# Another order of work in a hand-ordered attention pipeline

## The chip, the core and the metric

The kernel runs on one core of a Trainium2 chip. The metric is the device time of one execution in microseconds (us). Four engines compute: TensorE (PE; its weight loads are PEld), VectorE (DVE), ScalarE (ACT) and GpSimd (POOL). SyncE (SP) issues transfers. Matrix products land in PSUM, which has eight banks here; DVE and ACT read it, and everything else lives in SBUF. Each engine runs its own instructions in the order written and waits for the others by semaphores.

## What is computed

A model of four blocks over an input of 4 sequences of 512 tokens with 128 features, in fp32. The first three (a gated scan, a mixture of eight experts, a causal attention) are not touched. The last is six layers, each a local attention with 16 heads of 64 features, in windows of 32 tokens with the window before, and a feed-forward block. Cut to what matters:

```python
def attn_layer(x, Wqkv, qs, ksc, Wo):          # x: 4 x 512 x 128
    q, k, v = jnp.split(x @ Wqkv, 3, -1)       # to 16 heads of 64
    q = l2norm(q) * qs
    k = l2norm(k) * ksc
    q = q * cos * scale + rotate_half(q) * sin * scale
    k = k * cos * inv + rotate_half(k) * sin * inv
    sim = einsum(q, k) * 8                      # own window and the one before
    attn = softmax(where(mask, -max, sim))
    return einsum(attn, v) @ Wo

def ffn_layer(x, g, bln, W1, b1, W2, b2):
    xn = (x - mean) / sqrt(var + 1e-5) * g + bln
    a, gate = jnp.split(xn @ W1 + b1, 2, -1)    # 341 features each
    return a * gelu(gate) @ W2 + b2

for i in range(6):
    x = attn_layer(x, ...) + x
    x = ffn_layer(x, ...) + x
```

## The kernel before

The six layers are one stage. Its unit of work is a `Chunk`: 128 tokens of one sequence in one layer, 6 x 4 x 4 = 96 of them in the order layer, sequence, chunk. A chunk passes through five iterations of the loop at the end of `fused`: as `xe` it gets its queries, keys and values, as `xd` its scores and exponentials, as `xc` its weighted values, as `xb` the transposes of these, as `xa` the output product. So each iteration works on five chunks at once. The order of the calls in the loop is the order on every engine: after the loop each instruction is tied to the one before it on its engine.

What the calls do, with the names of the tiles as the profile shows them:

- `rotate(j)`, four times a chunk (j = 0, 1: queries, 2, 3: keys): one product `q` (128 x 512), on DVE two multiplications by the rotation's tables (`lt`, L547 and L551), on POOL their sum `ro`, on ACT the square `sq` (L558), on DVE its sums over each head `ss` (L559). `scale_keys` and `scale_queries` turn the sums into the factors `rk` and `rn` by a power on POOL (L569); the keys are multiplied by theirs there (L576).
- `window` and `turn(j, engine)`: the transposes `tp_r` of a rotated piece into `qT` or `kT`, with a copy out of PSUM.
- `scores(g)`, for two groups of eight heads: the mask as a product with the identity (L621) and the scores `ls` onto it (L630), the largest of each row `lm` (L637) and its scaled form `lnb` (L641).
- `exponentials(g, of)`: eight activations `lp` (L650).
- `flip(g, k, engine)`: four transposes `lpt` of the exponentials and a copy `lpT`.
- `weigh(g)`: the weighted values `lo` (L674), a reciprocal `lr`, and the division `on` (L680, L682).
- `lift(j)`: transposes `tp_on` and the copy `oT`.
- `values(j)`: the product `lv` and its copy `vr` on ACT. `spread` sends `vr` to `vk` by three transfers on SP.
- `project`: the output product `ly` (L698), added to the sequence `sA` on DVE (L704).

After the fourth chunk of a sequence its `feedforward` is put on a list; `advance()` in the loop runs it piece by piece over the next four iterations: transposes `tp_f`, a copy `fn` and the norm's statistics `st_f`, `mv_f`, `rs_f` (L115 to L118), then the normalisation (L123), then transposes `tp_fb` and `xn`, the gates `fg`, the other half `fa` in three steps, the output `fy`. The number k of the iteration says which of these fall into it.

PSUM is shared out by tags, with two tiles each: `mm` (one bank each: `q`, `lv`, `ly`, `fa`, `fy` and one gate), `tr` (one bank each: all transposes) and `S` (two banks each: `ls`, `lo` and two gates). A new tile takes a bank when the tile before it in that bank has been read. [...]

Of the kernel before, what the change touches and what calls it, by code (L numbers as in the profile page):

```python
# [66 lines left out]
def fused(ctx: ExitStack, tc: tile.TileContext, a: dict, out: bass.AP):  # L67
# [7 lines left out]
    def psum(tag, name):  # L75
        return pp.tile([P, 2, 512] if tag == "S" else [P, 512], F32, tag=tag, name=name)
# [10 lines left out]
    def chunks(x):  # L87
        return x.rearrange("p (c d) -> p c d", c=NC)
# [360 lines left out]
    with ExitStack() as stage:  # L449
# [68 lines left out]
        class Chunk:  # L518


            def __init__(self, n, l, b, c, w, last):
                self.l, self.b, self.c, self.w, self.last = l, b, c, w, last
                self.tag = f"{l}_{b}_{c}"
                self.xs = sA[b][:, c * P : (c + 1) * P]
                self.V = vr[n % 2]
                self.VK = vk[n % 2]
                self.ss = sm.tile([P, 2 * HEADS], F32, tag="ss", name=f"ss{self.tag}")
                self.rot = {}
                self.S = {}
                self.nb = {}  # L530
                self.P = {}
                self.pT = {}
                self.on = {}

            def rotate(self, j):

                tag = f"{self.tag}_{j}"
                q = psum("mm", f"q{tag}")
                nc.tensor.matmul(  # L539
                    q, lhsT=self.xs, rhs=self.w["qkv"][:, j * 512 : (j + 1) * 512],  # L540
                    start=True, stop=True,
                )
                cs = self.w["rot"][:, 2 * (j // 2), self.c, :]
                sn = self.w["rot"][:, 2 * (j // 2) + 1, self.c, :]
                t1 = wk.tile([P, 512], F32, tag="t1", name=f"lt1{tag}")
                t2 = wk.tile([P, 512], F32, tag="t2", name=f"lt2{tag}")
                nc.vector.tensor_tensor(  # L547
                    heads(t1), heads(q), cs[:, None, :].to_broadcast([P, 8, DH]), ALU.mult
                )
                sn = sn.rearrange("p (two d) -> p two d", two=2)  # L550
                nc.vector.tensor_tensor(  # L551
                    swapped(t2), swapped(q)[:, :, ::-1, :],
                    sn[:, None].to_broadcast([P, 8, 2, 32]), ALU.mult,
                )
                self.rot[j] = wk.tile([P, 512], F32, tag="rotd", name=f"ro{tag}", bufs=6)
                nc.gpsimd.tensor_tensor(self.rot[j], t1, t2, ALU.add)  # L556
                sq = wk.tile([P, 512], F32, tag="sq", name=f"sq{tag}")
                nc.scalar.activation(sq, q, AF.Square)  # L558
                nc.vector.tensor_reduce(  # L559
                    self.ss[:, j * 8 : j * 8 + 8], heads(sq), AX.X, ALU.add  # L560
                )

            def norms(self, j, name, square):
# [49 lines left out]
                    to = self.kT[:, 4 * j - 8 : 4 * j - 4, WIN:]  # L613
                move(engine, to, chunks(tp))

            def scores(self, g):

                gt = f"{self.tag}_{g}"
                S = psum("S", f"ls{gt}")[:, :, 0 : 4 * KB]
                for par in range(2):  # L620
                    nc.tensor.matmul(  # L621
                        S[:, par], lhsT=ident_h, rhs=bands[min(self.c, 1)], start=True, stop=False
                    )
                S = S.rearrange("p a (s k) -> p a s k", s=4)
                for s in range(4):
                    for blk in range(2):

                        for par in range(2):
                            lo, to = par * 64, blk * QB
                            nc.tensor.matmul(  # L630
                                S[to : to + QB, par, s, :],
                                lhsT=self.qT[lo : lo + 64, 4 * g + s, to : to + QB],
                                rhs=self.kT[lo : lo + 64, 4 * g + s, to : to + KB],
                                start=False, stop=s == 3,
                            )
                m = sm.tile([P, 4, 2], F32, tag="lm", name=f"lm{gt}")
                nc.vector.tensor_reduce(  # L637
                    m.rearrange("p s a -> p a s"), S, AX.X, ALU.max, negate=True
                )
                nb = sm.tile([P, 8], F32, tag="lnb", name=f"lnb{gt}")  # L640
                nc.vector.tensor_tensor(  # L641
                    nb, m.rearrange("p s a -> p (s a)"), self.rq[:, 8 * g : 8 * g + 8], ALU.mult
                )
                self.S[g], self.nb[g] = S, nb
# [22 lines left out]
            def weigh(self, g):  # L667
                gt = f"{self.tag}_{g}"
                o = psum("S", f"lo{gt}")[:, :, 0 : 4 * (DH + 1)]
                o = o.rearrange("p a (h d) -> p a h d", h=4)  # L670
                for i in range(8):
                    for blk in range(2):
                        to = blk * QB
                        nc.tensor.matmul(  # L674
                            o[to : to + QB, i // 4, i % 4, :],
                            lhsT=self.pT[g][:, i, to : to + QB],
                            rhs=self.VK[blk][:, 8 * g + i, :], start=True, stop=True,
                        )
                r = sm.tile([P, 2, 4], F32, tag="lr", name=f"lr{gt}")
                nc.vector.reciprocal(r, o[:, :, :, DH])  # L680
                self.on[g] = wk.tile([P, 512], F32, tag="on", name=f"on{gt}", bufs=4)
                nc.vector.tensor_tensor(  # L682
                    self.on[g].rearrange("p (a h d) -> p a h d", a=2, h=4), o[:, :, :, 0:DH],
                    r[:, :, :, None].to_broadcast([P, 2, 4, DH]), ALU.mult,
                )
# [8 lines left out]
            def project(self):  # L694
# [7 lines left out]
                for h in range(2):  # L702
                    to = half(self.b, h)[:, self.c * P : (self.c + 1) * P]
                    nc.vector.tensor_tensor(to, y[h * 64 : h * 64 + 64, :], to, ALU.add)  # L704

        def feedforward(l, b, w):

# [68 lines left out]
        def advance():  # L776
            if steps:
                try:
                    next(steps[0])
                except StopIteration:  # L780
                    steps.pop(0)

        def at(i):
            return made[i] if 0 <= i < len(made) else None

        for i in range(len(todo) + 4):
            if i < len(todo):
# [6 lines left out]
            if xd:  # L794
                xd.window()
            if xc:
                xc.flip(0, 0, nc.vector)
            if xe:
                xe.rotate(2)
            if xc:  # L800
                xc.flip(0, 1, nc.scalar)
            if xa:
                xa.project()
                if xa.c == NC - 1:
                    steps.append(feedforward(xa.l, xa.b, xa.w))
                k = (xa.c + 1) % NC
            if xd:
                xd.turn(2, nc.scalar)
            if xe:
                xe.rotate(3)  # L810
                xe.scale_keys()
            if xd:
                xd.turn(0, nc.scalar)
            if xc:
                xc.weigh(0)
            if xb:
                xb.lift(0)
            if xd:
                xd.scores(0)
            if xe:  # L820
                xe.rotate(0)
            if xd:
                xd.exponentials(0, range(8))
            if xc:
                xc.flip(1, 0, nc.vector)
            if k in (0, 2):
                advance()
            if xc:
                xc.flip(1, 1, nc.vector)
            advance()  # L830
            if xd:
                xd.turn(3, nc.scalar)
            if xe:
                xe.rotate(1)
                xe.scale_queries()
            if xd:
                xd.turn(1, nc.scalar)
            if xc:
                xc.weigh(1)
            if xb:  # L840
                xb.lift(1)
            if xd:
                xd.scores(1)
            if xe:
                xe.values(0)
            if xd:
                xd.exponentials(1, range(4))
            if k in (0, 2):
                advance()
            if xe:  # L850
                xe.values(1)
                xe.spread()
            if xd:
                xd.exponentials(1, range(4, 8))
        while steps:
            advance()

# [111 lines left out]
```

## Time and profile before

| | |
|---|---|
| median of 3 runs | 3016.34 us (3015.14 to 3021.13) |
| the profiled execution | 3016.47 us |
| its span, first to last instruction | 3014.7 us |
| mean granted TensorE clock | 0.933 of full speed |
| busy PE, DVE, ACT, POOL | 2558.3, 1950.1, 1476.6, 1401.7 us |
| first `ly` addition of the six layers | at 825.6 us |
| last `ly` addition | at 2974.7 us |

The table is read so: the layers take over two thirds of the span, and the 95 intervals between their first and last output products are 22.6 us each on average. Busy time counts an engine's instructions from start to end; for PE, whose products overlap, it is no measure of how much more it could do.

### The profile page before, as it was taken

To read this page: it belongs to the slowest core of one execution; us is meant where nothing else is said; L and a number is where in the kernel's file an instruction comes from. 1 tells how busy PE (TensorE), PEld (TensorE's weight loads), DVE (VectorE), ACT (ScalarE), POOL (GpSimd) and SP (SyncE) were. 2 spreads that over 40 slices of the span, in tenths; PEclk is the share of its full clock that TensorE was granted. 3 is DMA by queue.
4 is the path that set the end of the run, shared out by engine and by line. 5 is a ranking of instruction groups with operands and counts; after the bars stand their busy time and mean duration, and the time that the engine had idled before them with its cause. 6 is when DMAs were issued, how large, how long until landed. Compare 5 with 4: busy or idle time off the path is not lost.

```text
span 3014.7 us, 56751 instructions
## 1 busy us (share of the span) xinstructions
PE 2558.3 (85%) x22640; PEld 1679.1 (56%) x22640; DVE 1950.1 (65%) x4218; ACT 1476.6 (49%) x3417; POOL 1401.7 (46%) x1002
## 2 busy tenths in 40 slices
PE   3899888887779888888888898888888888988886
PEld 1567545554456555555555565555555555655553
DVE  6344466666676666766667666666666676666764
ACT  1111133333556555555555565555555555655553
POOL 2000011111766555665556555565655565555550
PEclk7799989999899999999999999999999999999998
DMA  5000000000112111121112111121111211111110
GB/s 168 1 1 1 1 1 1 1 1 1 42 32 77 32 31 33 42 67 33 31 40 67 33 42 31 31 68 41 32 32 32 75 34 31 41 32 31 37 37 17
DMA packets 44963, 103.92 MB, mean 34 GB/s; under 512 B 5526, under 2 KB 23196, under 8 KB 43804
## 3 DMA queue, kind: packets, MB, share of 16 engines
q1 hardware_dynamic: 41852, 97.27, 12.3%
q8 instruction: 178, 2.92, 0.4%
q10 hardware_dynamic: 2848, 3.03, 0.3%
q14 instruction: 85, 0.70, 0.1%
HBM read 25.75 MB, written 1.05 MB: 9 GB/s over the span
## 4 chain that ended last, share of the span: by engine, by line
PE 33%; DVE 22%; ACT 17%; issue 2%; ACTq 0%; DMA 0%; DVEq 0%; POOL 0%; POOLq 0%
PE q L539 7%; PE ly L698 6%; ACT lp L650 6%; PE lv L586 5%; DVE lt L547 5%; ACT sq L558 5%; PE tp_r L134 4%; DVE lt L551 4%; DVE ss L559 3%; PE ls L630 3%; DVE lm L637 3%; DVE on L682 2%; PE lo L674 2%; PE lpt L662 2%; PE tp_on L134 1%
## 5 line engine op out<-in xcount | busy, mean ns | idle before, releaser
L556 POOL TENSOR_TENSOR ro<-lt,lt 128x512 f32<-128x512 f32 x384 | 487.5, 1270 | 721.8 <-DVE lt L551 369.3
L558 ACT ACTIVATE sq<-q 128x512 f32<-128x512 f32 x384 | 232.1, 604 | 644.8 <-DVE lt L551 603.1
L650 ACT ACTIVATE lp<-ls,lnb,rn 128x96 f32<-128x96 f32 x1536 | 529.0, 450 | 4.1 <-DVE lnb L641 3.8
L559 DVE TENSOR_REDUCE ss<-sq 128x8 f32<-128x512 f32 x384 | 263.3, 686 | 352.4 <-ACT sq L558 352.4
L539 PE MATMUL q<-wqkv,sA 128*128 128x512 f32 x768 | 430.5, 644 | 4.7 <-DVE fh L738 2.9
L134 PEld LDWEIGHTS tp_r<-ident,ro 128*128 128x128 f32 x1536 | 197.6, 151 | 265.4 <-issue 156.0
L547 DVE TENSOR_TENSOR lt<-q,rot 128x512 f32<-128x512 f32 x384 | 265.4, 691 | 106.4 <-PE q L539 105.0
L134 PE MATMUL tp_r<-ident,ro 128*128 128x128 f32 x1536 | 254.8, 293 | 81.9 <-DVE st_f L115 48.1
L662 PEld LDWEIGHTS lpt<-ident,lp 128*96 128x96 f32 x1536 | 180.6, 130 | 242.3 <-issue 139.6
L569 POOL TENSOR_TENSOR rn<-rn,neg_half 128x16 f32<-128x16 f32 x96 | 278.9, 2905 | 64.9 <-DVE rn L566 64.8
L569 POOL TENSOR_TENSOR rk<-rk,neg_half 128x16 f32<-128x16 f32 x96 | 278.8, 2905 | 27.6 <-DVE rk L566 27.6
L662 PE MATMUL lpt<-ident,lp 128*96 128x128 f32 x1536 | 233.4, 282 | 64.0 <-DVE lpT L516 60.8
L551 DVE TENSOR_TENSOR lt<-q,rot 128x512 f32<-128x512 f32 x384 | 261.0, 680 | 0.0
L516 DVE COPY lpT<-lpt 96x512 f32<-96x512 f32 x288 | 192.0, 681 | 105.6 <-PE lpt L662 105.5
L630 PE MATMUL ls<-kT,qT 64*64 64x96 f32 x6144 | 185.7, 262 | 53.7 <-ACT qT L516 53.7
L674 PE MATMUL lo<-vk,lpT 96*64 96x65 f32 x6144 | 223.8, 225 | 1.1 <-ACT lpT L516 1.1
L630 PEld LDWEIGHTS ls<-kT,qT 64*64 64x64 f32 x6144 | 149.8, 142 | 128.3 <-issue 65.5
L698 PE MATMUL ly<-oT,lwo 128*128 128x128 f32 x1536 | 194.4, 280 | 26.9 <-ACT vr L590 26.9
L674 PEld LDWEIGHTS lo<-vk,lpT 96*64 96x64 f32 x6144 | 197.0, 138 | 35.7 <-issue 34.3
L586 PE MATMUL lv<-wqkv,sA 128*128 128x512 f32 x384 | 207.4, 644 | 3.2 <-ACT sq L558 3.2
L590 ACT COPY vr<-lv 128x512 f32<-128x512 f32 x192 | 113.8, 593 | 179.4 <-PE lv L586 179.4
L698 PEld LDWEIGHTS ly<-oT,lwo 128*128 128x128 f32 x1536 | 178.9, 192 | 37.8 <-ACT vr L590 32.5
(178 smaller groups left out, 4195.8 us busy)
## 6 DMA issues: line engine op xcount, KB each, us to landing
vk<-vr SPq DMA_DIRECT2D x96, 390.0 KB, 4.0
vk<-vr SPq DMA_DIRECT2D x96, 260.0 KB, 3.4
vk<-vr SPq DMA_DIRECT2D x72, 130.0 KB, 2.3
wqkv<-in_lwqkv_dram SPq DMA_DIRECT2D x6, 1536.0 KB, 10.0
ew<-in_ew_dram SPq DMA_DIRECT2D x16, 256.0 KB, 6.3
lwo<-in_lwo_dram SPq DMA_DIRECT2D x6, 512.0 KB, 10.9
lw<-in_lw_dram SPq DMA_DIRECT2D x6, 341.0 KB, 10.2
cst<-in_cst_dram ACTq DMA_DIRECT2D x1, 1028.0 KB, 5.3
```

Of the source, the lines that this page charges most:

```text
L134: nc.tensor.transpose(tp[:, c * P : (c + 1) * P], i[:, c, :], ident)
L539: nc.tensor.matmul(q, lhsT=self.xs, rhs=self.w["qkv"][:, j * 512 : (j + 1) * 512], start=True, stop=True,)
L547: nc.vector.tensor_tensor(heads(t1), heads(q), cs[:, None, :].to_broadcast([P, 8, DH]), ALU.mult)
L551: nc.vector.tensor_tensor(swapped(t2), swapped(q)[:, :, ::-1, :], sn[:, None].to_broadcast([P, 8, 2, 32]), ALU.mult,)
L556: nc.gpsimd.tensor_tensor(self.rot[j], t1, t2, ALU.add)
L558: nc.scalar.activation(sq, q, AF.Square)
L569: nc.gpsimd.tensor_tensor(r, r, neg_half.to_broadcast([P, HEADS]), ALU.pow)
L630: nc.tensor.matmul(S[to : to + QB, par, s, :], lhsT=self.qT[lo : lo + 64, 4 * g + s, to : to + QB], rhs=self.kT[lo : lo + 64, 4 * g + s, t ...
L650: nc.scalar.activation(self.P[g][:, i, :], self.S[g][:, i % 2, i // 2, :], AF.Exp, bias=self.nb[g][:, i : i + 1], scale=self.rq[:, 8 * g + ...
L662: nc.tensor.transpose(pt[0:KB, i * P : (i + 1) * P], self.P[g][:, 4 * k + i, :], ident)
L674: nc.tensor.matmul(o[to : to + QB, i // 4, i % 4, :], lhsT=self.pT[g][:, i, to : to + QB], rhs=self.VK[blk][:, 8 * g + i, :], start=True, ...
L698: nc.tensor.matmul(y, lhsT=self.w["o"][:, j, :], rhs=self.oT[:, j, :], start=j == 0, stop=j == INNER // P - 1,)
```

## The change

The loop calls the same work in another order, and several functions are cut in two so that their halves can be called apart.

- `rotate` is cut: `query(j)` does the product and its square, `rotate(j)` the rest. The square is now ahead of the two multiplications, and `query(3)` is called between `rotate(2)` and `rotate(3)`, ahead of `project`.
- `scores` is cut into `mask`, `scores` and `largest`; `weigh` into `weigh` and `divide`. The mask's product, the weighted values and the scores are called one after the other, and `lift` follows them. The mask's tile is now taken before that of the weighted values.
- `project` follows `turn(0)`. It puts the feed-forward on the list itself.
- The norm's statistics read the copy `fn` in SBUF, no longer `tp_f` in PSUM.
- The engine of the copies of `flip` and `turn(3)` depends on k. Over four iterations DVE had twelve copies of `flip` and ACT four; now DVE has nine and ACT seven. One of the four copies of `turn(3)` is on DVE.
- The second product of the values and all exponentials of the second group are at the end of the iteration.

```diff
-            def rotate(self, j):
+            def query(self, j):
                 tag = f"{self.tag}_{j}"
-                q = psum("mm", f"q{tag}")
+                self.q[j] = q = psum("mm", f"q{tag}")
                 nc.tensor.matmul(
                     q, lhsT=self.xs, rhs=self.w["qkv"][:, j * 512 : (j + 1) * 512],
                     start=True, stop=True,
                 )
+                self.sq[j] = wk.tile([P, 512], F32, tag="sq", name=f"sq{tag}")
+                nc.scalar.activation(self.sq[j], q, AF.Square)
+
+            def rotate(self, j):
+                tag, q = f"{self.tag}_{j}", self.q[j]
...
                 nc.gpsimd.tensor_tensor(self.rot[j], t1, t2, ALU.add)
-                sq = wk.tile([P, 512], F32, tag="sq", name=f"sq{tag}")
-                nc.scalar.activation(sq, q, AF.Square)
                 nc.vector.tensor_reduce(
-                    self.ss[:, j * 8 : j * 8 + 8], heads(sq), AX.X, ALU.add
+                    self.ss[:, j * 8 : j * 8 + 8], heads(self.sq[j]), AX.X, ALU.add
                 )
...
-            def scores(self, g):
-                gt = f"{self.tag}_{g}"
-                S = psum("S", f"ls{gt}")[:, :, 0 : 4 * KB]
+            def mask(self, g):
+                self.S[g] = S = psum("S", f"ls{self.tag}_{g}")[:, :, 0 : 4 * KB]
                 for par in range(2):
                     nc.tensor.matmul(
                         S[:, par], lhsT=ident_h, rhs=bands[min(self.c, 1)], start=True, stop=False
                     )
-                S = S.rearrange("p a (s k) -> p a s k", s=4)
+
+            def scores(self, g):
+                self.S[g] = S = self.S[g].rearrange("p a (s k) -> p a s k", s=4)
...
+            def largest(self, g):
+                gt, S = f"{self.tag}_{g}", self.S[g]
                 m = sm.tile([P, 4, 2], F32, tag="lm", name=f"lm{gt}")
...
+            def divide(self, g):
+                gt, o = f"{self.tag}_{g}", self.o
                 r = sm.tile([P, 2, 4], F32, tag="lr", name=f"lr{gt}")
...
-            stats = statistics(chunks(tp), f"f{tag}")
+            stats = statistics(n, f"f{tag}")
...
-            xa, xb, xc, xd, xe = (at(i - k) for k in (4, 3, 2, 1, 0))
-            k = (i - 4) % NC
...
+            xa, xb, xc, xd, xe = (at(i - k) or idle for k in (4, 3, 2, 1, 0))
+            k = (i - 3) % NC
+            xd.window()
+            xc.flip(0, 0, nc.vector)
+            xe.query(2)
+            xc.flip(0, 1, nc.vector if k in (1, 3) else nc.scalar)
+            xd.turn(2, nc.scalar)
+            xe.rotate(2)
+            xe.query(3)
+            xd.turn(0, nc.scalar)
+            xa.project()
+            xe.rotate(3)
+            xe.scale_keys()
+            xd.mask(0)
+            xc.weigh(0)
+            xc.divide(0)
+            xd.scores(0)
+            xd.largest(0)
+            xb.lift(0)
+            xe.query(0)
+            xd.exponentials(0, range(8))
+            xe.rotate(0)
             if k in (0, 2):
                 advance()
+            xc.flip(1, 0, nc.scalar if k in (0, 2) else nc.vector)
             advance()
+            xc.flip(1, 1, nc.vector if k == 1 else nc.scalar)
+            xd.turn(3, nc.vector if k == 1 else nc.scalar)
+            xe.query(1)
+            xd.turn(1, nc.scalar)
+            xe.rotate(1)
+            xe.scale_queries()
             if k in (0, 2):
                 advance()
+            xe.values(0)
+            xd.mask(1)
+            xc.weigh(1)
+            xc.divide(1)
+            xd.scores(1)
+            xd.largest(1)
+            xb.lift(1)
+            xe.values(1)
+            xe.spread()
+            xd.exponentials(1, range(8))
```

The removed loop had, for an iteration with all five chunks and without the tests for missing ones: `xd.window`, `xc.flip(0, 0, DVE)`, `xe.rotate(2)`, `xc.flip(0, 1, ACT)`, `xa.project`, `xd.turn(2)`, `xe.rotate(3)`, `xe.scale_keys`, `xd.turn(0)`, `xc.weigh(0)`, `xb.lift(0)`, `xd.scores(0)`, `xe.rotate(0)`, `xd.exponentials(0, 0..7)`, `xc.flip(1, 0, DVE)`, `advance` for k = 0 and 2, `xc.flip(1, 1, DVE)`, `advance`, `xd.turn(3)`, `xe.rotate(1)`, `xe.scale_queries`, `xd.turn(1)`, `xc.weigh(1)`, `xb.lift(1)`, `xd.scores(1)`, `xe.values(0)`, `xd.exponentials(1, 0..3)`, `advance` for k = 0 and 2, `xe.values(1)`, `xe.spread`, `xd.exponentials(1, 4..7)`; all `turn`s with ACT's copies. An iteration without some chunk skipped its calls by tests; in the changed loop an empty `Idle` object takes them.

More of the change, by code (lines that the diff above doesn't have):

```diff
@@ L527, in __init__ @@
                 self.ss = sm.tile([P, 2 * HEADS], F32, tag="ss", name=f"ss{self.tag}")
+                self.q = {}
+                self.sq = {}
                 self.rot = {}
@@ L643, in scores @@
                 )
-                self.S[g], self.nb[g] = S, nb
+                self.nb[g] = nb
                 self.P[g] = wk.tile([P, 8, KB], F32, tag="lp", name=f"lp{gt}")
@@ L669, in weigh @@
                 o = psum("S", f"lo{gt}")[:, :, 0 : 4 * (DH + 1)]
-                o = o.rearrange("p a (h d) -> p a h d", h=4)
+                self.o = o = o.rearrange("p a (h d) -> p a h d", h=4)
                 for i in range(8):
@@ L704, in project @@
                     nc.vector.tensor_tensor(to, y[h * 64 : h * 64 + 64, :], to, ALU.add)
+                if self.c == NC - 1:
+                    steps.append(feedforward(self.l, self.b, self.w))
         def feedforward(l, b, w):
@@ L781, in advance, with __getattr__ @@
                     steps.pop(0)
+        class Idle:
+            def __getattr__(self, name):
+                return lambda *of: None
+        idle = Idle()
         def at(i):
@@ L791, in fused @@
                 made.append(Chunk(i, l, b, c, ws[l], at(i - 1)))
-            xa, xb, xc, xd, xe = (at(i - k) for k in (4, 3, 2, 1, 0))
-            k = (i - 4) % NC
[L794 to L825, printed above, removed]
+            xa, xb, xc, xd, xe = (at(i - k) or idle for k in (4, 3, 2, 1, 0))
@@ L826, in fused @@
+            xb.lift(0)
+            xe.query(0)
+            xd.exponentials(0, range(8))
+            xe.rotate(0)
             if k in (0, 2):
                 advance()
-            if xc:
-                xc.flip(1, 1, nc.vector)
+            xc.flip(1, 0, nc.scalar if k in (0, 2) else nc.vector)
             advance()
[L831 to L847, printed above, removed]
+            xc.flip(1, 1, nc.vector if k == 1 else nc.scalar)
[4 more added lines that the diff above has]
+            xe.scale_queries()
@@ L848, in fused @@
             if k in (0, 2):
                 advance()
[L850 to L854, printed above, removed]
+            xe.values(0)
[8 more added lines that the diff above has]
+            xd.exponentials(1, range(8))
         while steps:
```

## The prediction

> **What bounds the kernel now.** I read the page's busy shares and slices first, then the busy times by stretch, then the waits, then the timeline. The stage that the change touches runs from about 780 us to the end, 96 chunks of tokens, and is even: slices 11 to 39 look alike.
>
> ```profile
> PE 2558.3 (85%) x22640; PEld 1679.1 (56%) x22640; DVE 1950.1 (65%) x4218; ACT 1476.6 (49%) x3417; POOL 1401.7 (46%) x1002
> ...
> PEclk7799989999899999999999999999999999999998
> ```
>
> TensorE is the fullest engine, yet not at its limit. The stretches show four chunks in a row, cut at the starts of `ls` of group 1 (columns: length, then busy PE, PEld, DVE, ACT, POOL, then the granted clock):
>
> ```profile
> 1523.83:1548.70 24.87, 19.56 (x205) 13.54 (x205) 17.17 (x41) 12.73 (x31) 14.39 (x11) 0.86 0.12 30
> 1548.70:1571.86 23.16, 20.81 (x212) 13.54 (x211) 14.64 (x31) 16.04 (x35) 13.43 (x11) 0.97 0.15 36
> 1571.86:1594.63 22.77, 20.24 (x206) 13.37 (x205) 15.09 (x27) 12.94 (x31) 12.86 (x9) 0.96 0.12 30
> ```
>
> With the chunk before them (1502.46 to 1523.83, 21.37 us) four chunks, a "round", take 92.17 us, and every round repeats it: the same transposes start at 1447.71, 1539.87 and 1632.02. I name the chunks by the k of the loop: k=0 (the feed-forward's norm) 24.87, k=1 (its gates) 23.16, k=2 (its other half) 22.77, k=3 (its output) 21.37. Who stops TensorE, from the waits of 1000 to 2900 us (total, times, longest):
>
> ```profile
> PE lpt L662 <- DVE lpT L516: 55.2, 20, 2.8
> PE tp_r L134 <- DVE st_f L115: 43.1, 19, 2.3
> PE ls L630 <- ACT qT L516: 39.3, 126, 0.6
> PE tp_on L134 <- ACT kT L516: 36.8, 20, 1.8
> PE ly L698 <- ACT vr L590: 25.7, 21, 1.3
> ```
>
> So once a round TensorE waits 2.8, 2.3, 1.8 and 1.3 us, and at most chunks' scores 0.3. Each long wait has a tail. The timeline of PE (start, length, tile, then the wait before it):
>
> ```profile
> 1536.07 0.60 PE L662 MATMUL lpt<-ident,lp 128*96 128x128 f32 x4
> 1536.51 0.60 PE L134 MATMUL tp_f<-ident,sA 128*128 128x128 f32 x4
> 1539.87 1.09 PE L662 MATMUL lpt<-ident,lp 128*96 128x128 f32 x4 [2.76 <-DVE lpT L516]
> 1543.23 1.09 PE L134 MATMUL tp_r<-ident,ro 128*128 128x128 f32 x4 [2.27 <-DVE st_f L115]
> 1544.11 1.92 PE L539 MATMUL q<-wqkv,sA 128*128 128x512 f32 x2
> 1545.82 0.96 PE L134 MATMUL tp_r<-ident,ro 128*128 128x128 f32 x4
> 1546.71 1.15 PE L674 MATMUL lo<-vk,lpT 96*64 96x65 f32 x32
> ...
> 1552.22 1.02 PE L539 MATMUL q<-wqkv,sA 128*128 128x512 f32 x2
> ```
>
> Four transposes take 0.60 us when PE has run on (`lpt` at 1536.07) and 1.09 after the wait, a `q` pair 1.02 and 1.92: half speed, until about 1546.4, shortly before `lo`. After the round's 1.84 us (up to 1570.28) it comes again, until about 1573.8; after its 1.27 us (up to 1578.57) it does not.
>
> [...] `sq` (L558) reads the `q` that L551 reads, and waited for it 603.1 us in all. [...] The trace has 0.53 us from the start of `tp_r` to that of `lo` (another mode) against 0.43 from `tp_r` to `q` (the same): about 0.1 a change.
>
> **The change part by part.** Durations below are start to start, from the timeline of 1500 to 1595 us: DVE's 512-wide operations 0.61 (0.69 to their end), `lm` 1.05, `lr` 0.23, eight exponentials 2.52, `sq` 0.63 until DVE goes on, `lv` to its copy 1.16, `q` to its square 1.13; PE: `tp_on` 0.50, `tp_r` 0.45 (0.53 ahead of `lo`), `q` 0.86, `lv` 0.88, `ly` 1.88, mask 0.44, `lo` 1.09, `ls` 0.82.
>
> *Squares first.* DVE's wait `ss <- sq` goes (15.0 us in the waits of one round). But now L547 can only start when `sq` is done, and `sq` of piece 2 stands in ACT's order behind the eight exponentials of group 1. The banks of the changed program, as built, say who waits for that: `ly`, moved behind `rotate(2)`, lies in the bank of that `q`; before, it lay in the bank of `lv`. From the end T of a chunk's last `ls`: `lv` starts at 0.50, its copy at 1.66, the exponentials at 2.14 (`lnb` is there at 1.6), `sq` at 4.66, L547 at 5.29, L551 from 5.90 to 6.58, **`ly` at 6.65**. TensorE has had only 4.93 us of work by then (0.50, 0.88, `lpt` 0.44, `q` 0.86, `lpt` 0.44, `tp_r` 0.45, `q` 0.86, `tp_r` 0.50): a **new wait of 1.2 to 1.7 us in every chunk** (where ACT copies the second half of `lpT`, k even, most of it falls on the `tp_r` ahead of `ly`, whose bank that copy, queued behind the square, must free). Queued behind `ly`: all of PE, and on DVE its two additions, then everything.
>
> *From `ly` on* DVE sets the pace. `ly` ends its issue at 8.53, DVE adds at 8.75 (0.55), rotates piece 3 (3 x 0.61), `rk` 0.17, `lr` and `on` 0.84, `lm` at 12.12, `lnb` 13.17, rotates piece 0 from 13.28 (1.83), copies `lpT` at 15.11, done 15.80. `tp_r` of piece 3 needs that bank: 15.87. Then `tp_r` 0.45, `q` 0.86, `tp_r` 0.53, `lv` 0.88, mask 0.44, `lo` 1.09, `ls` 0.82: 5.07, so k=3 ends at **20.94**. Its feed-forward product (2.6) hides: PE is free at 15.73.
>
> *Copies dealt by turn.* k=1 has three of them on DVE, so ACT goes from exponentials (13.51 to 16.19) to the table load 1.28 and three gates at 0.6: 19.3; `lv` takes their bank then, +3.23: **22.6**. k=2: `lpT` on ACT behind the exponentials, 16.03 to 16.60; `tp_r` 16.67, `q` 17.12, its square 18.25, L547 and L551 until 20.17; `lv`, in that `q`'s bank, at 20.24: **23.5**.
>
> *Norm from SBUF.* k=0: `fn` is copied behind the exponentials at 16.03; the bank is free at 16.66 and no longer after 1.92 us more of statistics. Reading SBUF costs the same (`st_z` 268 ns, `st_f` 274). But PE waits from 13.1 to 16.7 for `fn`, and statistics until 18.6, POOL's power 1.02, L123 1.12, end 20.97, then `tp_fb` and 3.23: **24.4**.
>
> *Mask, weighted values, scores side by side.* The wait for `qT` (1.9 us in that round) goes: `qT` is there at 7.5, `ls` starts at 10.1. One mode change in four goes, 0.1 each, and of it only the second group's lies on the chain: under 0.4 a round, within my rounding. POOL has 13.3 us a chunk of 22 and is early everywhere (`ro` of piece 0 ends at 18.0, wanted in the next chunk); SP issues the same three transfers behind the same `vr`, at 2.3, and `lo` wants them two chunks on: nothing, unless they came a whole chunk late.
>
> Sum: 24.4 + 22.6 + 23.5 + 20.9 = **91.4 against 92.17**, but at full clock, where the 92.17 holds two half-clock stretches. It is a floor for these durations: each term is a chain in the engines' written order. What the half clock adds I can only bound. Below, 0: the waits at `ly` are 1.2 to 1.7, between the 1.27 that was not throttled and the 1.84 that was. Above, 7.5: all four `ly` at half speed, 1.88 each. k=0's wait of 3.6 is throttled for sure, but the norm covers it. I take 1.7 a round, as one `ly` in four at half speed costs 1.9 and some of it falls after `ly` where DVE is later anyway: 93.1, +0.9 x 23 rounds = +21, and +3 for the four chunks before any feed-forward, which take 20.19 now and 20.9 to 21.5 then. On the profiled execution's 3016.47 us (its span 3014.7; the median of the runs is 3016.34): **3040 us**.
>
> **Rivals.** (1) Not slower: the clock holds at `ly`. Then 91.4: 3016.5 - 0.8 x 23 + 3 = 3001 us. For it: 1.27 us never throttled; the side is decided where the half clock costs 0.7 us a round, a third of one `ly`. Against: 1.7 is nearer 1.84. (2) No change: [...] In the trace of before the first wait of the rounds comes at 987.26, 1079.25, 1171.32, 1263.44 and so on: 91.99, 92.07, 92.12 apart, then 92.15 and no more, [...] 3017 to 3020. (3) Every `ly` at half speed: 98.9, about 3175. (4) PE runs dense: the round less its 11.3 us of listed waits, 23 x 11.3 = 260, gives 2757. For it: 15 us of DVE's waits go. Against: the chain through `sq` and `ly` is longer than such a round.
>
> **Numbers.** Forecast slower, 3022 to 3090: 0.4; (3) and what lies between: 0.1; (2) 0.17; (1), my sums being up to 1.5% too long: 0.31; (4) 0.02. 0.2% is about what a measurement of this kernel tells from no change. Range 2985 to 3110: it leaves out a tenth above and less below.
>
> **What would show it.** Right: a wait `ly <- DVE lt` of over 1 us in nearly every chunk, `ss <- sq` and `st_f` gone, `tp_r <- lpT` or DVE in its place, rounds of 91 to 95 us. Wrong: `ly` without a wait, or rounds under 90.

## The result, and the profile after

| | before | after |
|---|---|---|
| median | 3016.57 us | **3118.26 us** (3115.35 to 3122.05, 4 runs) |
| ratio | | 1.0335, 95% interval 1.0317 to 1.0353 |
| the profiled execution, its span | 3016.47, 3014.7 us | 3122.05, 3119.9 us |
| mean granted clock | 0.933 | 0.945 |
| first to last addition of `ly` | 2149.1 us | 2252.1 us |

The change makes the kernel 3.4% slower, and nearly all of it lies in the layers: their interval is 103.0 us longer, the whole span 105.2. (The median of before holds one run more than the table ahead.) The forecast was 3040 us, with a range up to 3110. The page after, busy shares and granted clock:

```profile
PE 2519.2 (81%) x22640; PEld 1667.1 (53%) x22640; DVE 2025.8 (65%) x4170; ACT 1521.5 (49%) x3465; POOL 1402.8 (45%) x1002
...
PEclk7799898999999999999999999999999999999898
```

TensorE is less full than before (2519.2 us busy against 2558.3) and its clock is higher (0.945 against 0.933), so the loss is waiting, not slower products. From one start of `tp_f` to the next a round took 91.83 to 92.18 us before, 92.13 on average over the first twenty. After, it takes 95.47 to 95.49 in most rounds (95.48 below) and 97.2 or 97.6 in some, 96.13 on average: +4.0, and these twenty rounds are 80 of the 105 us. Busy times by stretch of one typical round after, cut as in the prediction, for k=0, 1, 2, 3 (length, busy PE, PEld, DVE, ACT, POOL, granted clock, DMA share, GB/s):

```profile
1559.99:1584.88 24.89, 19.32 (x213) 13.66 (x209) 17.55 (x39) 14.56 (x33) 14.98 (x11) 0.93 0.13 33
1584.88:1608.15 23.27, 19.60 (x209) 12.84 (x206) 16.02 (x30) 14.24 (x31) 12.56 (x10) 1.00 0.14 36
1608.15:1633.89 25.74, 19.81 (x211) 12.70 (x207) 16.91 (x29) 14.58 (x32) 15.00 (x11) 1.00 0.11 27
1633.89:1655.48 21.59, 19.11 (x210) 12.88 (x206) 16.09 (x28) 12.27 (x29) 11.37 (x9) 1.00 0.15 38
```

No chunk got its forecast (24.4, 22.6, 23.5, 20.94); k=2 is off by most. The granted clock is 1.00 in three of the four and 0.93 in k=0. The rounds of 97.2 and 97.6 differ from this one in k=2 (27.47 and 27.12) and in the k=0 between them (25.63); k=1 and k=3 are the same in every round. TensorE's waits of 1000 to 2900 us after (total, times, longest):

```profile
PE tp_r L134 <- ACT lpT L516: 83.7, 59, 2.7
PE lpt L672 <- ACT fn L726: 81.5, 20, 4.1
PE ly L711 <- ACT qT L516: 69.6, 40, 1.8
PE fa L750 <- DVE lt L558: 32.4, 20, 1.8
PE lv L591 <- ACT fh L744: 29.8, 20, 1.5
```

The long waits of before (`lpt` for `lpT`, `tp_r` for `st_f`, `tp_on` for `kT`) are no longer among them, and new ones stand behind ACT: `tp_r` three times a round, `ly` twice, `lpt` once for `fn`. Now the middle of k=3 after, one round earlier, from the timeline of all engines (start, length, engine, line; then the wait before it):

```profile
1545.15 0.68 DVE L558 TENSOR_TENSOR lt<-q,rot 128x512 f32<-128x512 f32 x1
...
1545.97 2.02 PE L711 MATMUL ly<-oT,lwo 128*128 128x128 f32 x16 [1.77 <-ACT qT L516]
...
1548.04 0.59 DVE L717 TENSOR_TENSOR sA<-ly,sA 64x128 f32<-64x128 f32 x2 [1.61 <-PE ly L711]
...
1549.87 0.68 DVE L564 TENSOR_REDUCE ss<-sq 128x8 f32<-128x512 f32 x1
1550.10 1.27 POOL L563 TENSOR_TENSOR ro<-lt,lt 128x512 f32<-128x512 f32 x1 [2.85 <-DVE lt L558]
...
1550.58 0.82 DVE L571 TENSOR_SCALAR rk<-ss 128x16 f32<-128x16 f32 x1
...
1551.31 0.20 DVE L693 RECIPROCAL lr<-lo 128x8 f32<-128x8 f32 x1
```

`ly` starts 6.75 us after the chunk's start (T = 1539.22), where 6.65 was forecast, after a wait of 1.77. The view names `qT`, which `ly` does not read; L558, the last reader of the bank that `ly` takes, ends at 1545.83, 0.06 before that copy. (That `ly` waits for the bank follows from the order in which the tiles are taken; the view alone does not show it.) DVE then waits 1.61 for `ly`. And `rk`, 174 to 177 ns in every instance before, takes 0.82: it ends at 1551.40, when POOL's `ro` ends (1551.37). So it is in 95 of the 96 chunks: `rk` ends 0.03 us after the `ro` beside it. The same place before:

```profile
1512.52 0.60 ACT L558 ACTIVATE sq<-q 128x512 f32<-128x512 f32 x1 [1.73 <-DVE lt L551]
...
1513.15 0.69 DVE L559 TENSOR_REDUCE ss<-sq 128x8 f32<-128x512 f32 x1 [0.72 <-ACT sq L558]
...
1513.87 0.17 DVE L566 TENSOR_SCALAR rk<-ss 128x16 f32<-128x16 f32 x1
```

There DVE stood 0.72 us before `ss`. POOL's `ro` ran from 1512.57 to 1513.84, in that wait and beside `ss`, and `rk` found it over. The wait that the change was credited with removing had covered `ro`. With the square done early `ss` follows L558 at once, and `rk` comes while `ro` still runs.

In k=2, ACT's timeline shows what else is late:

```profile
1513.65 0.59 ACT L595 COPY vr<-lv 128x512 f32<-128x512 f32 x1 [0.28 <-PE lv L591]
1514.25 1.28 ACT L660 ACT_TABLE_LOAD   x1
1515.55 2.69 ACT L660 ACTIVATE lp<-ls,lnb,rn 128x96 f32<-128x96 f32 x8
1518.09 0.64 ACT L546 ACTIVATE sq<-q 128x512 f32<-128x512 f32 x1
1518.57 0.60 ACT L516 COPY lpT<-lpt 96x512 f32<-96x512 f32 x1
```

The chunk before used Gelu, and a table load of 1.28 us stands ahead of the eight exponentials (in e2, without Gelu, it is gone); the square and the copy `lpT` behind them come that much later, and `tp_r` waits 2.67 for that copy.

### The profile page after: what moved, and what is told of

It is laid out like the page before. It is cut to its first block, busy times and chain, and to the rows that moved or that the text cites. A ratio compares the mean times of both kernels' runs of the same rounds, so it can differ in the third digit from the quotient of the medians.

```text
span 3119.9 us, 56778 instructions
## 1 busy us (share of the span) xinstructions
PE 2519.2 (81%) x22640; PEld 1667.1 (53%) x22640; DVE 2025.8 (65%) x4170; ACT 1521.5 (49%) x3465; POOL 1402.8 (45%) x1002
## 4 chain that ended last, share of the span: by engine, by line
PE 30%; ACT 22%; DVE 21%; issue 3%; POOL 0%; DMA 0%; DVEq 0%; ACTq 0%; POOLq 0%
ACT lp L660 13%; PE ly L711 7%; PE lv L591 6%; DVE lt L554 4%; DVE lt L558 4%; PE lo L684 3%; PE q L541 3%; PE tp_r L134 3%; DVE lm L647 3%; ACT sq L546 3%; PE ls L636 3%; DVE rk L571 2%; DVE ss L564 2%; DVE on L695 2%; PE tp_on L134 2%
## 5 line engine op out<-in xcount | busy, mean ns | idle before, releaser
L660 ACT ACTIVATE lp<-ls,lnb,rn 128x96 f32<-128x96 f32 x1536 | 517.3, 445 | 98.5 <-DVE lnb L651 98.0
L705 ACT COPY oT<-tp_on 128x512 f32<-128x512 f32 x192 | 112.7, 587 | 668.7 <-PE tp_on L134 668.7
L541 PE MATMUL q<-wqkv,sA 128*128 128x512 f32 x768 | 416.6, 626 | 1.0 <-DVE lt L558 1.0
L672 PE MATMUL lpt<-ident,lp 128*96 128x128 f32 x1536 | 240.2, 281 | 90.2 <-ACT fn L726 85.8
L711 PE MATMUL ly<-oT,lwo 128*128 128x128 f32 x1536 | 211.1, 295 | 90.8 <-ACT qT L516 81.5
L546 ACT ACTIVATE sq<-q 128x512 f32<-128x512 f32 x384 | 239.4, 624 | 88.9 <-PE q L541 88.9
L558 DVE TENSOR_TENSOR lt<-q,rot 128x512 f32<-128x512 f32 x384 | 261.4, 681 | 0.0
L711 PEld LDWEIGHTS ly<-oT,lwo 128*128 128x128 f32 x1536 | 194.1, 205 | 111.6 <-ACT qT L516 49.0
L581 POOL TENSOR_TENSOR ro<-ro,rk 128x512 f32<-128x512 f32 x192 | 196.3, 1044 | 7.5
L516 DVE COPY lpT<-lpt 96x512 f32<-96x512 f32 x216 | 145.7, 683 | 62.6 <-PE lpt L672 58.9
L647 DVE TENSOR_REDUCE lm<-ls 128x8 f32<-128x768 f32 x192 | 182.0, 948 | 2.1 <-PE ls L636 2.1
```

The lines of the kernel that those rows point to most:

```text
L541: nc.tensor.matmul(q, lhsT=self.xs, rhs=self.w["qkv"][:, j * 512 : (j + 1) * 512], start=True, stop=True,)
L546: nc.scalar.activation(self.sq[j], q, AF.Square)
L558: nc.vector.tensor_tensor(swapped(t2), swapped(q)[:, :, ::-1, :], sn[:, None].to_broadcast([P, 8, 2, 32]), ALU.mult,)
L660: nc.scalar.activation(self.P[g][:, i, :], self.S[g][:, i % 2, i // 2, :], AF.Exp, bias=self.nb[g][:, i : i + 1], scale=self.rq[:, 8 * g + ...
L672: nc.tensor.transpose(pt[0:KB, i * P : (i + 1) * P], self.P[g][:, 4 * k + i, :], ident)
L711: nc.tensor.matmul(y, lhsT=self.w["o"][:, j, :], rhs=self.oT[:, j, :], start=j == 0, stop=j == INNER // P - 1,)
```

## The experiments

**Is it the square behind the exponentials?** e3: the exponentials of group 1 are called one iteration later, behind the square of piece 2 and the copy of `lpT`.

```diff
             xe.spread()
-            xd.exponentials(1, range(8))
...
             xc.flip(0, 1, nc.vector if k in (1, 3) else nc.scalar)
+            xc.exponentials(1, range(8))
             xd.turn(2, nc.scalar)
```

> The changed kernel with the exponentials of the second group called in the next iteration, after query(2) and flip(0, 1), so that the square of piece 2 is ahead of them on ACT; nothing else moves, and the banks stay as they are. Theory 1: the square starts at T + 3.0 instead of T + 4.7 (T + 5.9 in the chunk after the gates), ly at T + 5.0 without a wait, everything behind it 1.7 us earlier in three chunks of four, nearer 0.5 in the one with the table load, where qT is late next: about -6 us a round, -140 us, 2980 us. Theory 2 (ly waits for its own operands or the mask, weighted values and scores side by side cost the time): ly waits as before, 3118 us. Theory 3 (half speed): as theory 1 in kind, but no less than the before's 3016.

**2981.41 us** (2978.01 to 2984.76), 0.9880 of before (0.9865 to 0.9895). TensorE's waits, of which two lines are enough:

```profile
PE lpt L672 <- ACT fn L726: 77.5, 19, 4.4
...
PE ly L711 <- DVE lt L558: 13.7, 41, 0.3
```

`ly` now waits 0.3 us at most, `tp_r` hardly for `lpT` any more; rounds alternate between 89.16 and 91.7. So the queue behind the eight exponentials costs 137 us of the changed order; without it the order is faster than before. It also takes away the later `lpT` and the table load ahead of the square, so the 137 are not those of `ly` alone. In k=1 and k=3, where DVE copies that `lpT` and no table is loaded ahead of the square, a chunk gets 1.4 us shorter (23.28 to 21.89, 21.59 to 20.15), by as much as the wait at `ly` falls there (from 1.7 and 1.8 to 0.3).

**Is it `rk`?** e1 and e8 move `scale_keys`, e1 behind `largest(0)`, e8 behind `divide(0)`, by when POOL's `ro` is all but over. The edit of e8:

```diff
             xe.rotate(3)
-            xe.scale_keys()
             xd.mask(0)
             xc.weigh(0)
             xc.divide(0)
+            xe.scale_keys()
             xd.scores(0)
             xd.largest(0)
```

> The changed kernel, with scale_keys called after largest(0) instead of straight after rotate(3); nothing else moves. Theory 1 (the loss is a chain of handoffs; in it rk, an operation of 16 columns, takes 0.82 us because it starts while POOL's sum ro runs and ends when that ends): rk falls to about 0.17 us, lm and all behind it come 0.65 us earlier in each chunk, 2.6 us a round, 23 rounds: about -60 us against the changed kernel, 3058 us, and the wait tp_r <- lpT shrinks. Theory 2 (rk is slow by itself, or DVE is not on the chain): rk stays 0.82, or the time stays within 10 us of 3118. Theory 3 (the loss is half-speed stretches of TensorE): no change either, as the long waits stay.

> The changed kernel with one edit: scale_keys is called behind divide(0) instead of behind rotate(3), as in e7_and_keys_later, but with the wait at ly left in. Theory 1 (DVE's chain from ly runs through rk, 0.82 us where POOL's ro holds it and 0.17 behind on): each of the four chunks 0.65 shorter, rounds of 92.9 instead of 95.5, 3050 to 3070 us, and no wait for the norm's power as in e1_keys_later (3090 us), since rk stands 1.1 us earlier than there. Theory 2 (POOL's order matters, not DVE's): as e1, 3080 to 3095 us. Theory 3 ([...]): anything under 3020 us.

e1: 3089.95 us (1.0247, 1.0230 to 1.0264). e8: **3047.94 us** (1.0109, 1.0092 to 1.0126). The groups of e8 (line, busy us, mean ns, idle before):

```profile
L571 DVE TENSOR_SCALAR rn<-ss 128x16 f32<-128x16 f32 x96 | 78.1, 813 | 3.3
...
L571 DVE TENSOR_SCALAR rk<-ss 128x16 f32<-128x16 f32 x96 | 16.3, 170 | 0.1
```

`rk` is back at 170 ns; `rn`, which was left where it was, directly behind its `ss`, keeps its 813. e8's rounds are 93.70, 93.73, 92.46 in turn, 93.4 on average over twenty: 2.7 less than after, against four times 0.65 = 2.6 expected, and 70 us in all. The short ones, by stretch (k=0, 1, 2, 3):

```profile
1718.79:1742.99 24.20, 18.22 (x213) 12.63 (x209) 16.91 (x39) 14.46 (x33) 15.05 (x11) 1.00 0.14 34
1742.99:1765.50 22.51, 19.32 (x211) 12.84 (x207) 15.23 (x30) 14.24 (x31) 12.50 (x10) 1.00 0.15 37
1765.50:1790.45 24.95, 19.80 (x211) 12.69 (x207) 16.15 (x29) 14.58 (x32) 14.98 (x11) 1.00 0.11 28
1790.45:1811.26 20.81, 19.04 (x210) 12.88 (x206) 15.33 (x28) 12.27 (x29) 11.37 (x9) 1.00 0.16 39
```

Each chunk is 0.7 to 0.8 us shorter than in the typical round after: where it now stands, `rk` takes almost nothing from DVE's chain. In the other two rounds of three `ly` of k=2 runs in part at half speed (3.0 to 3.4 us), and that takes 1.2 to 1.3 us back.

e1 gives 28 us only. Its k=1 and k=3 are as short as e8's (22.41 and 20.80), but `rk` is 1.1 us later still, POOL's power of the keys with it, and the norm's power waits behind that one: `tp_fb` waits up to 2.3 us for `fn` in fourteen rounds, in e8 up to 1.2. k=0 takes 26.12 on average, where after has 24.99.

**The table of Exp.** e2 replaces Gelu by Relu, so it computes something else and serves for its time alone:

```diff
-                    hT[0:fn, k, :], gate[0:fn, :], AF.Gelu, bias=vcol(V_B1 + l * 6 + 3 + k, fn)
+                    hT[0:fn, k, :], gate[0:fn, :], AF.Relu, bias=vcol(V_B1 + l * 6 + 3 + k, fn)
```

> The changed kernel with Relu in place of Gelu in the feed-forward's gates, which changes what is computed and takes away the two table loads a round (1.28 us each). Theory 1: in the chunk after the gates the load of the exponentials' table stands ahead of the second group's exponentials, the square behind them and so ly; without it that chunk is 1.3 shorter, and the load ahead of the gates, which lv waits for, another 1.3: -2.6 us a round, about -60 us, 3058 us. Theory 2 (tables are hidden behind ACT's idle time, it has 49% busy): 3118 within 10 us. Theory 3 (half speed): the 2.7 us wait in that chunk falls below 1.84 us, so the half-speed ly of 3.4 us seen once in four rounds goes too, some 8 us more.

3045.22 us (1.0089, 1.0074 to 1.0104), rounds of 92.55 in the main, 2.9 less than the 95.48 of after; on average 92.86, 3.3 less. Two loads of 1.28 go, not one: that ahead of the exponentials in k=2 (24.30 instead of 25.73; the longest `tp_r <- ACT lpT` falls from 2.7 to 1.2) and that ahead of the gates in k=1 (21.82 instead of 23.28), behind which `lv` waited 1.5 (this wait is gone); k=3 does not change. The other 0.4 of the 2.9 is not traced. Only the first load was missing in the prediction; the second is in its 22.6.

**The norm from SBUF.** e5 puts the statistics back on PSUM:

```diff
-            stats = statistics(n, f"f{tag}")
+            stats = statistics(chunks(tp), f"f{tag}")
```

> The changed kernel with the norm's statistics read from PSUM again, as before the change; the order stays. Theory 1: the bank of tp_f is held 1.9 us longer, so lpt waits 6.0 us instead of 4.1 once a round, but tp_fb waits for the norm anyway: +0.1 to +1 us a round, 3118 to 3140 us. Theory 2 (this part of the change costs time, [...]): faster than 3110 us.

3176.48 us (1.0528, 1.0513 to 1.0544): 58 us slower than the changed kernel, more than expected. Rounds are 98.98 each. `lpt` in k=0 waits up to 4.5 instead of 4.1, the transposes behind it wait again, and the half clock then reaches to `tp_fb`: 13.97 us from `tp_f` to the next scores of group 1 instead of 11.83. Of the 2.9 a round, on average, 2.1 lie there, in k=0, and 0.9 in k=2, where `ly` is at half speed (3.47 us) in every round and not only in some. Within the new order this part of the change is a clear gain, but much of it goes through the clock (0.933 granted on average, against 0.945).

**The deal of the copies.** e9 deals them as before, whatever k:

```diff
-            xc.flip(0, 1, nc.vector if k in (1, 3) else nc.scalar)
+            xc.flip(0, 1, nc.scalar)
...
-            xc.flip(1, 0, nc.scalar if k in (0, 2) else nc.vector)
+            xc.flip(1, 0, nc.vector)
...
-            xc.flip(1, 1, nc.vector if k == 1 else nc.scalar)
-            xd.turn(3, nc.vector if k == 1 else nc.scalar)
+            xc.flip(1, 1, nc.vector)
+            xd.turn(3, nc.scalar)
```

> The changed kernel with the copies dealt as before it: flip(0, 0) on DVE, flip(0, 1) on ACT, both flips of group 1 on DVE, all turns on ACT, whatever k. Theory 1 (the deal by turn shifts only where the wait behind the square lands): in k=1 and k=3 the second half of lpT now also stands behind the square on ACT, 0.5 us later than on DVE, so their tp_r and ly come 0.5 later; in k=0 and k=2 DVE's two copies take the place of ACT's behind the exponentials, at the same time within 0.5; in k=1 ACT gets the turn back, 0.5 later. Together +1 to +2 a round: 3130 to 3165 us. Theory 2 (the deal by turn is what costs): rounds shorter by 1 us or more, under 3095 us.

3170.49 us (1.0520, 1.0504 to 1.0536), a little above the expected end: the deal by turn, too, is a gain of 52 us here. Rounds are 98.98, as in e5. But the reason expected did not show, and that the size came near was luck: k=1 and k=3 keep their length (23.19 and 21.55). The loss is in k=0 (27.23; 24.99 after, on average), where `tp_r` now waits 1.43 for DVE's copy `lpT`, and in k=2 (27.02 against 26.23), where `ly` takes 3.45 in every round. The granted clock of the whole run is 0.933, after's 0.945.

**The mask.** e10 puts it behind the division:

```diff
-            xd.mask(0)
             xc.weigh(0)
             xc.divide(0)
+            xd.mask(0)
             xd.scores(0)
```

(the same for group 1)

> The changed kernel with one edit: mask(g) is called behind divide(g), directly ahead of scores(g), and so takes its tile after that of the weighted values, as before the change. Theory 1 (side by side is worth little: 0.1 us a change of mode, and the second group's alone on the chain): +0 to +0.5 us a round, 3115 to 3135 us. Theory 2 (the mask, ahead of DVE's work, hides behind a wait, and behind lo it stands in the chain of lm): +0.4 us in up to four chunks, 3135 to 3160 us. Theory 3 (the order of the tiles matters: the mask's tile must wait for an earlier reader): faster, under 3110 us.

3140.60 us (1.0414, 1.0399 to 1.0430). The total speaks for theory 2, the trace for theory 1: rounds alternate between 95.88 and 98.68. The shorter is 0.40 above 95.48, four changes of mode at 0.1: with the mask, a product of tile 128*128, behind `lo`, of 96*64, the tile changes once more, and from the start of `ly` to that of `ls` it is 3.47 against 3.37. The longer loses 2.8 more in two half-clock stretches: in k=0 behind the wait for `fn` (26.2 instead of 25.0 us) and in k=2, where `ly` is at half speed behind the 2.67 wait at `tp_r`. The timeline of TensorE in e10, `ly` in k=2 of a short and of a long round:

```profile
1528.34 2.05 PE L711 MATMUL ly<-oT,lwo 128*128 128x128 f32 x16 [0.23 <-DVE lt L558]
```

```profile
1625.49 3.59 PE L711 MATMUL ly<-oT,lwo 128*128 128x128 f32 x16 [0.23 <-DVE lt L558]
```

After has such a long `ly` too (3.44 or 3.76 us), in two rounds of five. That it is more frequent with the later mask is seen; why was not tested.

**The square ahead, alone.** e4 makes this one edit in the kernel before; e12 adds the move of `scale_keys` behind `weigh(0)`, which holds the division there.

```diff
+                sq = wk.tile([P, 512], F32, tag="sq", name=f"sq{tag}")
+                nc.scalar.activation(sq, q, AF.Square)
                 cs = self.w["rot"][:, 2 * (j // 2), self.c, :]
...
-                sq = wk.tile([P, 512], F32, tag="sq", name=f"sq{tag}")
-                nc.scalar.activation(sq, q, AF.Square)
```

> The kernel before with one edit: in rotate, the square (and so its place in ACT's order and the first reading of q's bank) stands ahead of the two multiplications; the order of the calls, the banks and everything else are those of before. Theory 1 (the damage is done by what queues behind the square, and here the product behind it in that bank is q of piece 3, not ly): piece 2's square still stands behind ACT's exponentials of group 1, of which before only four are at the end of the chunk, so q of piece 3 and all of PE behind it wait up to 1 us a chunk, while DVE saves its wait ss <- sq (15.0 us a round). The two about cancel: rounds of 91 to 94 us, 2990 to 3060 us. Theory 2 (the square ahead is good by itself, and only the other parts of the change cost): DVE's saved waits show, rounds under 90 us, under 2970 us. Theory 3 (the square ahead carries the whole loss): rounds of 95 us and more, 3090 us and more.

> e4_square_alone (the kernel before with the square ahead of the multiplications, 3020 us, rounds of 92.15, rk and rn at 0.82 us) with one more edit: scale_keys is called behind weigh(0), which holds the reciprocal and the division, so that rk is free of ro. Theory 1 (the square ahead saves DVE's waits, and rk held by ro gives part of that back on the chain): 0.3 to 0.65 us in each chunk, rounds of 89.5 to 91, 2955 to 2990 us. Theory 2 ([...] 92.15, as in the kernel before and in e4): 3010 to 3025 us.

e4: 3019.78 us (1.0014, 1.0007 to 1.0022). e12: **2961.66 us** (0.9823, 0.9808 to 0.9837). In e4 rounds stay at 92.15, but not their parts: k=1 is 1.0 us shorter, k=2 and k=3 0.2 each, and k=0 1.3 longer (26.19), as the half clock reaches `lo` there (2.00 us instead of 1.15). The largest of DVE's waits of 1000 to 2900 us, of before, then of e4 (total, times, longest):

```profile
DVE ss L559 <- ACT sq L558: 308.7, 330, 2.4
```

```profile
DVE lt L549 <- ACT sq L544: 409.5, 245, 3.9
```

The square ahead does not take DVE's wait away; it moves it from `ss` to `lt` (which waited another 85.9 for `q` before). And it makes `rk` 812 ns in e4 as in the changed kernel. e12 takes that back (170 ns) and rounds fall to 89.4 to 90.6, 2.3 less on average: 1.0 in k=1 to k=3 together, 1.3 in k=0. So with `rk` out of the way the square ahead is a gain in the old order, where four exponentials stand ahead of it and a `q`, not `ly`, waits behind it. How much of the 1.3 in k=0 is `rk` and how much the half clock, which e4 alone had longer, is not separated; nor was `scale_keys` moved without the square.

**A better order.** e6 is e3 with the feed-forward's first piece ahead of the exponentials of group 0 when k = 0; e7 adds the move of e8; e11 also moves `scale_queries` behind `divide(1)`.

```diff
+            if k == 0:
+                advance()
             xd.exponentials(0, range(8))
             xe.rotate(0)
-            if k in (0, 2):
+            if k == 2:
                 advance()
```

> The changed kernel with the exponentials of group 1 put behind the square of the next chunk (as in e3_square_before_exp, 2981 us, rounds of 90.4 on average), and one more edit: for k = 0 the first piece of the feed-forward (tp_f, fn, statistics) is called ahead of the exponentials of group 0. Theory 1 (the chain of k=0 runs through fn, which stands behind eight exponentials on ACT): the wait lpt <- fn of 4.1 us goes or falls under 2, and with it the half clock behind it; k=0 gets 2 to 2.5 us shorter, rounds of 88, 2920 to 2935 us. Theory 2 (k=0 is bound by DVE, which then has the statistics before the second rotation of queries): no gain, 2975 to 2990 us.

> e6_norm_copy_earlier with one more edit: scale_keys is called behind divide(0), so that DVE's rk stands behind lr and on, by when POOL's ro of piece 3 is over. Theory 1 (rk is held by POOL's ro until that ends, 0.65 us in every chunk, on the chain that sets the end): rk takes 0.17 us again, 2 to 2.6 us a round less than e6, 45 to 60 us faster than it. Theory 2 (with the ly wait gone the chain no longer runs through rk): the same as e6 within 10 us. Theory 3 (the power on POOL comes later and pushes the norm's power, as in e1_keys_later): a gain of under 30 us, with a wait tp_fb <- DVE fn of about 2 us in half of the rounds.

> e7_and_keys_later (2877 us, rounds of 85.75) with one more edit: scale_queries is called behind divide(1), so that rn too stands behind on. Theory 1 (rn, 0.82 us while ro of piece 1 runs, is on the chain of group 1's largest values in chunks where DVE ends last): 0.65 us in two to four chunks, rounds of 83 to 84.5, 2820 to 2850 us. Theory 2 (in the second half TensorE runs on and DVE has slack): within 10 us of 2877.

e6: 2969.69 us (0.9843, 0.9829 to 0.9858), only 12 less than e3. The wait moved: `lpt <- fn` falls from 4.4 to 0.7, but the exponentials come later, and ACT's copies of `lpT` behind them. The timeline of TensorE in e6, k=0:

```profile
1521.23 0.64 PE L672 MATMUL lpt<-ident,lp 128*96 128x128 f32 x4 [0.35 <-ACT fn L726]
1524.92 1.12 PE L134 MATMUL tp_r<-ident,ro 128*128 128x128 f32 x4 [3.05 <-ACT lpT L516]
```

**e7: 2876.75 us** (0.9544, 0.9530 to 0.9558), 93 less than e6 where 45 to 60 was expected; rounds of 85.75 in the main, on average 3.9 less. In k=1 and k=3 a chunk is 0.77 shorter, as in e8, which would make 3.1 for four. The rest goes with shorter waits: that `tp_r` waits 2.38, and `fa` in k=2 1.16 instead of 1.93; `fa` is at full speed then in every round (1.10 us), where e6 has 1.8 to 1.9 in seven of twenty. e7's page:

```profile
PE 2477.9 (86%) x22640; PEld 1644.0 (57%) x22640; DVE 1985.9 (69%) x4170; ACT 1525.6 (53%) x3465; POOL 1400.9 (49%) x1002
```

e11: 2875.14 us (0.9535, 0.9520 to 0.9549), no different from e7, though `rn` falls from 818 to 175 ns. In the second half of a chunk DVE has slack.

## Why the prediction was right or wrong

**The new wait at `ly`: right.** Time (6.75 against 6.65), length (1.7 to 1.8 against 1.2 to 1.7), cause and consequence are as worked out; for even k most of it falls on `tp_r`, 1.26 and 2.67 us. The exception is k=2: behind the table load `ly` comes at 8.1. e3 shows that the queue behind the exponentials decides the sign. Of the signs named, the waits came; the rounds, at 95.48 and more, lie outside of 91 to 95.

**`rk` 0.17: the step that failed.** It made the chunks' chains too short. The price came from a row of before, where `ro` was over by the time of `rk`. The prediction booked the end of the wait `ss <- sq` as DVE's saving and did not ask what had run meanwhile. With 0.82, k=3 becomes 20.94 + 0.65 = 21.59, which is what was measured, and k=1 22.6 + 0.65 = 23.25 against 23.27. k=0 is 0.49 above its forecast. In all 2.6 a round at most; e8 has it by experiment, 2.7 a round. And with `rk` out of the way the chains of the prediction fit: e8's stretches are 24.20, 22.51 and 20.81 where 24.4, 22.6 and 20.94 was forecast, and 24.95 in k=2, where 23.5 and the load of the next point make 24.8. Why `rk` takes 0.82 beside `ro` and ends with it, and 0.17 behind it, is not shown by the traces; the reduction `ss` beside the same addition keeps its 0.68.

**k=2 23.5: a term was left out.** The sum had 2.52 us for eight exponentials in every chunk. In k=2 the table load comes first: 1.28. With it and `rk` 23.5 becomes 25.4, against 25.74; the other 0.3 is not traced. e2, without the load, has 24.30. In ACT's timeline the load starts 0.01 after the copy before it ends, and the exponentials 1.30 after the load starts: nothing but the load of 1.28 is seen, so that is what counts.

**The sum.** 91.4 + 2.6 + 1.3 = 95.3, against 95.48 in a typical round. The floor itself, chains in the engines' written order, held; two of its terms were too small.

**Half clock 1.7: too large.** What comes on top of the typical round is 96.13 - 95.48 = 0.65 on average. The waits of 1.7 to 1.8 ahead of `ly` stayed without it (2.02 us); only the 2.67 in k=2 has it, in two rounds of five, and the stretch behind k=0's 4.07 is longer in one of five. By luck this error hid part of the others. Rival (3), every `ly` at half speed, is refuted by the same rows, though its 3175 us lies nearer to the measured time than the forecast does. Rival (2), rounds that stay at the 92.15 of before, did not come: they take 95.47 and more. What held them at 92.15 before is not shown by any run.

**Norm, deal: not nothing.** The prediction described both but did not price the new order without them. e5 and e9 put 58 and 52 us on them; each, taken back, brings a round to 98.98, with the half clock in k=0 and k=2 of every round (`ly` of k=2 takes 3.47 and 3.45; the granted clock is 0.933 in both runs). How much is the edits' own cost and how much the clock's is not separated, and the two need not add up.

**Mask under 0.4 a round: right as to its own cost** (0.40), but not as to the clock that goes with it (22 us in all).

**The first chunks, +3: too small.** The first `tp_f` starts at 899.5 us against 892.1, so 7.4 are lost ahead of the first feed-forward. The twenty rounds add 80.1 and the last layer, up to its last `ly`, 17.2: in all 104.7 of the 105.2 us by which the profiled span grew.

## What to carry to other kernels

Before you count a wait as saved, list what other engines do during it: the stall of 0.72 us kept a small DVE operation clear of POOL, and without it the operation grew by nearly as much on the chain (0.17 to 0.82). An early operation is early only if its engine's queue is free: a square put ahead in the program, but behind eight exponentials in ACT's order, took a wait from one operation of DVE and put one on DVE's next and on TensorE. And a reordering that loses may be near one that wins: with the exponentials behind the square the same edits run at 0.988 of before, with the norm's copy earlier and `rk` behind the division at 0.954.

## What the hardware showed that was not expected

- A DVE operation on 128x16 elements, `rk`, takes 0.82 us instead of 0.17 while POOL's addition `ro` runs, and then ends 0.03 us after it (95 of 96 chunks after); behind the addition it takes 0.17 again (e8). The reduction `ss` ahead of it, over 512 elements a partition and beside the same addition, keeps its 0.68.
- Edits that move work inside a round can leave its length as it is: in e4 chunks change by up to 1.3 us each, and the round stays at the 92.15 of before; e5 and e9, with different edits, both come to 98.98. What holds these lengths is not shown; no run isolates it.
